# Two-layer convolutional attention on one Trainium2 core: layer 1's last product from seven block products, and its scores in five PSUM banks a unit

## The chip, the cores and the metric

The kernel runs on one core of one Trainium2 chip, in one launch. The metric is the device time of the launch in microseconds (us). Three runs of the kernel before took 3203.37, 3204.1 and 3202.24 us; the median is 3203.37. The five engines that the profile names are PE (TensorE, matmuls), DVE (VectorE), ACT (ScalarE), POOL (GpSimd) and SP (SyncE, which here only issues DMAs). Matmul results land in PSUM, whose banks hold 512 float32 numbers in each of 128 partitions.

## The reference

The input x has 8 images of 512 channels and 32 × 32 = 1024 positions, all float32. Two layers run one after the other; image by image they are:

```
# layer 0
h = group_norm(x)                                # 32 groups
q, k, v = split(w_qkv h + b_qkv)                 # 8 heads of 64 channels
a = softmax((q k) / sqrt(64)) v                  # 1024 x 1024 in each head
x = x + group_norm(w_proj a + b_proj)
# layer 1, weights normalized row by row
qkv = w_qkv x
q, k, v = split(qkv / (sqrt(mean(qkv^2 over channels)) + 1e-4))
attn = softmax(q k / sqrt(512))                  # one head, 1024 x 1024
x = (x + w_out (attn v)) / sqrt(2)
```

The change is all in layer 1's two large products: the scores q·k, and the last product, attn times (w_out v).

## The kernel before

**Stages.** The images go one after the other through the same stages, and one image's last stage is drawn into the next one's first. Layer 0 of an image is 32 steps (`STEPS`, line 370), each a block of 128 rows in two heads. `Heads.step` (line 636) orders a step: two maxima on DVE and two exponentials on ACT (`softmax`), the values of an earlier step, the **fills** (PE work of something else, as functions in a list), the scores of the next step, the transposition of the last step's exponentials on DVE with its four DMAs on SP (`turn`), the **earlies**, the reciprocal and POOL's scaling (`scale`), the **laters**. Then come the output projection and its group norm (`finish_layer0`), and layer 1 (`Layer1`, line 921). The weights of q and k are folded into one matrix ("score"), those of w_out and v into another ("value"), once at the start.

**Layer 1.** `Layer1.project` makes, in this order: products with the Gram matrix for the norms; u = score matrix times x (two `score_unit`s); v = (value matrix times x) turned (four `value_unit`s); and the exponentials of the scores, e (four `weight_unit`s). All matmuls of these units are 512 (value: 256) columns wide and 128 rows deep. The tiles e[0] and e[1] hold the two halves of the 1024 query positions, with eight blocks of 128 key positions each. POOL adds the exponentials up in `esum`. After `project` come the column totals (`square_sums`, `total`: a transposition, a small matmul, a reciprocal, and a round trip through DRAM on SP) and the last product, which is scaled by the reciprocal totals and added to x (`keep`).

**Seven block products.** Every unit computes a 2 × 2 block product from seven products of block sums in place of eight (class `Seven`, line 759). The sums on the left are S1 to S4, on the right T1 to T4 (`RightSide`, line 722). Each product is two calls of PE.matmul that accumulate in one PSUM bank, four MATMUL instructions in the trace. Two products share one two-bank tile from the pool `ps_s` (three tiles, `wide`, line 111); when the second is done, both are drained, by copies on ACT or additions on DVE into the result. The other pool, `ps_m`, has two single banks (`bank`, line 114). A unit of scores has seven drains on DVE and one on ACT; then ACT takes the exponential in place.

**The last product** is a plain one: for each half `th` of the positions and each block `c` of 128 channels, eight PE.matmuls of 512 columns (`products`, line 1096). The half 0 and block 0 of half 1 run before the next image's first scores; blocks 1, 2 and 3 of half 1 are the fills of the next image's steps 0, 1 and 2, with their `keep`s as laters (lines 1447 and 1448). Blocks 2 and 3 are made in 64-row halves into two banks (`products_rows`, line 1105), since the scores of layer 0 around them are 64-row matmuls too; `keep` joins the halves with a copy on ACT and two operations on POOL.

**Order.** `InOrder` (line 26) pins every instruction to program order on its engine, so the engines run exactly what the program lists, in that order. That is why every instruction in the profile has line L34, and groups are told apart by tiles: `p_e_B` and `p_e_T` are the PSUM tiles of the weight units, `po<-e,v` is the last product, `s<-qk` layer 0's scores, `pq` the projections of q and k. Waits between engines are put in by the framework from the tiles that are read and written.

**Around the change.** `project_seven` (line 476) makes q and k of a head pair of layer 0 in pieces, as fills; its products use the small banks too. Its weights come by `fetch_qk` (line 257) into the tile `qk7`, issued on SP: j = 1 and 2 after the score units (lines 1058 to 1060), j = 3 and 4 at steps 8 and 16. `Sums` (line 434) builds the sums for it, on DVE, one a product of weight units 1 to 3 (lines 1073 to 1076). The input of the image after next is loaded (`load_x`) and its group norm is reckoned between the parts of the last product (lines 1410 to 1443).

Of the kernel before, what the change touches and what calls it, by code (L numbers as in the profile page):

```python
# [13 lines left out]
P = 128  # L14
# [38 lines left out]
def attention_blocks_kernel(  # L53
# [157 lines left out]
    def rsqrt(r, v, n, name):  # L211
# [6 lines left out]
        "qk": ("qk", [P, 2, CI, C]), "score": ("qk", [P, 7, 2, CH]), "qk7": ("qk", [P, 2, 14, P]),  # L218
# [27 lines left out]
    def place(name, b):  # L246
        tag, shape = places[name]
        near[name] = weights.tile(shape, F32, tag=f"w_{tag}", name=f"{name}_{b}")
        if name == "v":

            near["v7"] = near[name]
            flat = near[name].rearrange("p k h c -> p (k h c)")
            near["v#"], near["v_"] = flat[:, CI * C :], flat[:, : CI * C]
            near[name] = flat[:, : CI * C].rearrange("p (ci c) -> p ci c", ci=CI)
        return near[name]

    def fetch_qk(j, b):

        if j == 1:
            place("qk7", b)  # L260
# [215 lines left out]
    def project_seven(b, j, right):  # L476
# [3 lines left out]
        qk = pair.tile([P, 2, N], F32, tag="qk", name=f"qk_{b}_{j}")  # L480
        kp = qk[:, 1, :].rearrange("p (be m) -> p be m", be=4)
# [5 lines left out]
        q1, q2 = (qk[:, 0, th * HN : (th + 1) * HN] for th in range(2))  # L487
        k1, k2 = (kp[:, :, th * P : (th + 1) * P] for th in range(2))

        def add(to, a, b_):  # L490
            return lambda: PO.tensor_add(to, a, b_)

        adds = (
            ([], []),
            ([], []),
            ([add(q2, q2, q1), add(k2, k2, turned(q2))], [add(k1, k1, k2), add(k2, k2, turned(tmp[1]))]),
            ([add(q1, q1, tmp[0]), add(q2, q2, tmp[1])], [add(q2, q2, tmp[2])]),
        )

        def pieces():  # L500
# [3 lines left out]
            yield adds[0]  # L504
# [17 lines left out]
        return qk, pieces()  # L522
# [398 lines left out]
    class Layer1:  # L921
# [10 lines left out]
        def project(self, hn_next):  # L932
# [96 lines left out]
            def weight_unit(m):  # L1029
# [7 lines left out]

                c = {f"{th + 1}{i + 1}": e[th][:, m + 4 * i, :] for i in range(2) for th in range(2)}

                def last(which):  # L1040
                    th, t = int(which[0]) - 1, m + 4 * (int(which[1]) - 1)
                    et, esum = c[which], self.sums[:, halves_[th]]
                    AC.activation(et, et, AF.Exp, bias=shift, scale=rinv[:, t : t + 1])
# [6 lines left out]
                return Seven(f"e_{b}_{m}", HN, left, self.right(slice(m * P, (m + 1) * P)), c, last, swap=True)  # L1050

            done = ([], [])
            for m in range(2):
                for k, _ in enumerate(score_unit(m).steps()):
                    if (m, k) == (0, 3):
                        roots()
                        broadcast()
            if b + 1 < B:
                for j in (1, 2):
                    fetch_qk(j, b + 1)  # L1060
# [6 lines left out]
            more = iter(())  # L1067
            if b + 1 < B:
                place("v", b + 1)
                self.next = Sums(b + 1, hn_next)  # L1070
                more = self.next.steps()
                next(more)
            for m in range(4):
                for _ in weight_unit(m).steps():
                    if m:
                        next(more, None)
            Seven.drain()
            Seven.half = None
            slots.give(f"u_{b}")

# [7 lines left out]
        def total(self):  # L1088

            pe = ps_s.tile([P, SQ], F32, tag="sc", name=f"pe_{self.b}")  # L1090
# [5 lines left out]
        def products(self, th, c, between=None, po=None):  # L1096
            po = self.po[th, c] = bank(f"po1_{self.b}_{th}_{c}") if po is None else po
            e = self.e[th]

            terms = [(self.v[:, t, c * P : (c + 1) * P], e[:, t, :]) for t in (0, 4, 1, 5, 2, 6, 7, 3)]  # L1100
            for k, _ in enumerate(matmuls(po, terms)):
                if k == 1 and between:
                    between()

        def products_rows(self, c):


            pos = self.po[1, c] = [bank(f"po1_{self.b}_1_{c}_{r}") for r in range(2)]
            for t in range(NT):
                for r in range(2):  # L1110
                    rows = halves[r]
                    PE.matmul(
                        pos[r],
                        self.v[rows, t, c * P : (c + 1) * P],
                        self.e[1][rows, t, :],
                        start=(t == 0),
                        stop=(t == NT - 1),
                    )

        def keep(self, th, c):  # L1120

            hs = slice(th * HN, (th + 1) * HN)

            po, rest = self.po.pop((th, c)), None
            if isinstance(po, list):
                po, rest = po
            share = near["v#"][:, N : N + HN] if self.b + 1 < B else po
            VE.tensor_mul(share, po, self.sums[:, hs])
            VE.scalar_tensor_tensor(self.xt[:, c, hs], self.xt[:, c, hs], 2.0 ** -0.5, share, ALU.mult, ALU.add)
            if rest is not None:  # L1130
                part = near["v#"][:, :HN]
                AC.copy(part, rest)
                PO.tensor_mul(part, part, self.sums[:, hs])
                PO.tensor_add(self.xt[:, c, hs], self.xt[:, c, hs], part)
            if th == 1:
                SY.dma_start(out=ov[self.b, :, c, :], in_=self.xt[:, c, :])

        def last_piece(self, c, cols):

            hs, po = slice(HN + cols.start, HN + cols.stop), bank(f"po1_{self.b}_1_{c}_{cols.start}", HN // 2)  # L1140
            run(matmuls(po, [(self.v[:, t, c * P : (c + 1) * P], self.e[1][:, t, cols]) for t in range(NT)]))
            VE.tensor_mul(po, po, self.sums[:, hs])
            VE.scalar_tensor_tensor(self.xt[:, c, hs], self.xt[:, c, hs], 2.0 ** -0.5, po, ALU.mult, ALU.add)
            SY.dma_start(out=ov[self.b, :, c, hs], in_=self.xt[:, c, hs])
# [134 lines left out]
    laters = [[] for _ in range(CI)]  # L1279
    heads.scores(0)  # L1280
    for b in range(B):
        hn, more = heads.hn, b + 1 < B
        todo, due, rest = iter(()), [], []
        for i in range(STEPS):
# [12 lines left out]
            if i < CI:  # L1297
                fill, later = fills[i] + fill, laters[i]
# [3 lines left out]
            if r == 0:  # L1302
                if j + 1 < CI:
                    heads.qk[j + 1], todo = project_seven(b, j + 1, one.next.right) if b else project_rows(
                        b, j + 1, hn, near["v#"]
                    )
# [30 lines left out]

            if b and i == NB:
# [78 lines left out]
        one.square_sums()  # L1417

        for c in range(CI):
            if c % 2 == 0:  # L1420
                po = wide(f"po1_{b}_0_{c}")
            one.products(0, c, norm_step if c == CI - 1 else None, po[:, c % 2])
            if c == 0:
                one.total()
                if b + 2 < B:
                    for ci in range(2, CI):
                        load_x(b + 2, hn_next, ci)
            if c and b + 2 < B:

                for ci in range(CI)[2 * c - 2 : 2 * c]:  # L1430
                    for k in range(2):
                        norm1.stats(ci, k)
                if c == 2:
                    norm1.aggregate()
            if c == CI - 1:
                norm_step()
            if c % 2:
                one.keep(0, c - 1)
                one.keep(0, c)
        slots.give(f"e_{b}_0")  # L1440
        if more:
            one.products(1, 0, norm_step)
            run(steps)
            one.keep(1, 0)
# [50 lines left out]
```

## Time and profile before

| what | value |
|---|---|
| median of three runs | 3203.37 us (3202.24 to 3204.1) |
| span of the profiled execution | 3197.2 us |
| instructions in it | 36929 |
| one weight stage (four units), image 0 | 404 to 452 us |
| its last product before the next scores | 452 to 487 us |
| the next image's steps 0 to 3 | from 487 us |

The times of steps come from one profiled execution, whose span is a little shorter than the time of a run. A line of a timeline has the start in us, the length in us, the engine, the line, the operation, the tile that it writes and (after the arrow) the tiles that it reads, its shape, and how many instructions are drawn together; in brackets stands how long the engine had been idle before it, and which engine ended that. A line of the costliest groups has the sum of the busy time, the mean of one in ns, and the idle time just before them with what ended most of it. A row of the windows has the stretch, its length, the busy time of PE, weight load, DVE, ACT and POOL (instructions in brackets), the granted PE clock (1.00 is full), the share of the DMA engines, and GB/s. On one engine, the time from one start to the next is the price of an instruction in a row; its length in the trace includes a tail that overlaps with the next.

### The profile page before, as it was taken

How to read it: one execution, taken by the hardware profiler on the slowest of the kernel's cores; microseconds unless marked ns; L12 is line 12 of the kernel's file. 1: busy time of each engine (PE TensorE's matmuls, PEld its weight loads, DVE VectorE, ACT ScalarE, POOL GpSimd, SP SyncE). 2: the span in 40 equal slices, each digit the busy share in tenths (PEclk: the TensorE clock that was granted, in tenths of full speed). 3: DMA queues.
4: the chain of work that ended last, by engine and by line, in shares of the span. 5: the costliest groups of instructions: out<-in, count | busy, mean ns of one | idle time of the engine just before them, and what ended most of it. 6: DMA issues, size and time to landing. Idle time of an engine off the chain costs nothing.

```text
span 3197.2 us, 36929 instructions
## 1 busy us (share of the span) xinstructions
PE 3172.7 (99%) x13374; PEld 1639.4 (51%) x13374; DVE 2286.3 (72%) x3175; ACT 1044.1 (33%) x1810; POOL 1269.7 (40%) x1033
## 2 busy tenths in 40 slices
PE   9999999999999999999999999999999999999899
PEld 5455644556444554445544555445554456444454
DVE  5697767866678766886658866687666877578753
ACT  2453124521145211551215512254023531245310
POOL 1554225732267212761226603366224642246121
PEclk9999999999999999999999999999999999999999
DMA  6777225862268511884128832388224872158600
GB/s 204 209 204 221 76 56 156 220 199 60 56 179 234 178 40 60 210 229 146 48 82 220 225 116 46 112 217 230 93 56 118 218 225 76 30 152 215 191 7 33
DMA packets 225853, 451.59 MB, mean 141 GB/s; under 512 B 21604, under 2 KB 62344, under 8 KB 219912
## 3 DMA queue, kind: packets, MB, share of 16 engines
q1 hardware_dynamic: 225552, 449.20, 50.1%
q8 instruction: 107, 1.75, 0.2%
q14 instruction: 74, 0.61, 0.1%
q10 hardware_dynamic: 120, 0.02, 0.0%
HBM read 137.26 MB, written 29.56 MB: 52 GB/s over the span
## 4 chain that ended last, share of the span: by engine, by line
PE 95%; DMA 2%; DVE 1%; SPq 1%; POOL 1%; issue 0%; ACT 0%; DVEq 0%; POOLq 0%
PE po L34 27%; PE s L34 14%; PE pq L34 7%; PE p_e_T L34 7%; PE p_v_T L34 6%; PE p_e_B L34 5%; PE p_v_B L34 5%; PE pqk L34 5%; PE py L34 4%; PE p_u_T L34 3%; PE p_o_T L34 3%; PE p_u_B L34 3%; PE p_o_B L34 2%; DMA pT<-pb 1%; PE pv L34 1%; PE pG L34 1%
## 5 line engine op out<-in xcount | busy, mean ns | idle before, releaser
L34 POOL TENSOR_SCALAR p<-p,tt 128x1024 f32<-128x1024 f32 x512 | 567.6, 1122 | 728.1 <-DVE tt L34 718.5
L34 ACT ACTIVATE p<-s,nm 128x1024 f32<-128x1024 f32 x512 | 566.2, 1111 | 821.8 <-DVE nm L34 498.4
L34 DVE TENSOR_REDUCE nm<-s 128x1 f32<-128x1024 f32 x512 | 602.5, 1218 | 147.3 <-PE s L34 146.5
L34 DVE STREAM_TRANSPOSE pb<-p 128x2048 f32<-128x2048 f32 x256 | 589.9, 2304 | 39.5 <-DMA pT<-pb 21.6
L34 PE MATMUL s<-qk 64*128 64x512 f32 x2048 | 501.9, 603 | 0.2
L34 PE MATMUL po<-pT,v 128*64 128x256 f32 x4096 | 473.4, 382 | 2.7 <-DMA pT<-pb 2.6
L34 PE MATMUL po<-e,v 128*128 128x512 f32 (+2 forms) x1264 | 449.5, 588 | 0.0
L34 PEld LDWEIGHTS po<-pT,v 128*64 128x64 f32 x4096 | 283.7, 137 | 228.4 <-issue 27.3
L34 PEld LDWEIGHTS po<-e,v 128*128 128x128 f32 (+1 forms) x1264 | 196.3, 189 | 233.9 <-issue 233.1
L34 PEld LDWEIGHTS s<-qk 64*128 64x128 f32 x2048 | 191.6, 186 | 235.5 <-issue 216.7
L34 PE MATMUL pq<-hn,qk 64*128 64x512 f32 (+1 forms) x420 | 191.8, 593 | 0.0
L34 POOL TENSOR_TENSOR esum<-esum,e 128x512 f32<-128x512 f32 x96 | 130.5, 1361 | 154.3 <-ACT e L34 151.8
L34 POOL TENSOR_TENSOR x<-x,o 128x1024 f32<-128x1024 f32 x21 | 52.2, 2514 | 348.9 <-ACT o L34 348.9
L34 POOL TENSOR_TENSOR u<-u,xy 128x512 f32<-128x512 f32 x64 | 79.2, 1270 | 278.6 <-DMA xy<-far_rinv 274.1
L34 ACT ACTIVATE e<-e,shift,rinv 128x512 f32<-128x512 f32 x128 | 101.1, 814 | 256.5 <-DVE e L34 256.5
L34 DVE TENSOR_TENSOR e<-e,p_e_T 128x512 f32<-128x512 f32 x160 | 107.0, 685 | 86.4 <-PE p_e_T L34 84.2
L34 DVE TENSOR_TENSOR v<-v,p_v_T 128x256 f32<-128x256 f32 x300 | 114.4, 419 | 68.9 <-PE p_v_T L34 49.9
L34 PE MATMUL pqk<-hn,qk 64*128 64x512 f32 (+1 forms) x672 | 158.2, 590 | 0.0
L34 PE MATMUL pq<-v,qk 64*128 64x512 f32 x336 | 150.9, 589 | 0.0
L34 PE MATMUL pq<-t,qk 64*128 64x512 f32 x336 | 150.9, 589 | 0.0
L34 PE MATMUL p_e_T<-s,t 128*128 128x512 f32 x320 | 147.8, 592 | 0.0
L34 PE MATMUL py<-x,gram 128*128 128x512 f32 x320 | 141.6, 602 | 4.4 <-DVE x L34 4.4
(224 smaller groups left out, 4116.5 us busy)
## 6 DMA issues: line engine op xcount, KB each, us to landing
pT<-pb SPq DMA_DIRECT2D x1024, 256.0 KB, 4.5
qk<-far_qk SPq DMA_DIRECT2D x21, 896.0 KB
hn<-in_x_dram SPq DMA_DIRECT2D x32, 512.0 KB, 4.5
x<-in_x_dram SPq DMA_DIRECT2D x32, 512.0 KB, 3.7
out_dram<-x SPq DMA_DIRECT2D x31, 512.0 KB, 3.1
score<-far_score SPq DMA_DIRECT2D x8, 1792.0 KB
value<-far_value SPq DMA_DIRECT2D x8, 1792.0 KB
proj<-far_proj SPq DMA_DIRECT2D x7, 1792.0 KB
```

The costliest lines, as they stand in the source:

```text
L34: return lambda *args, **kw: self._pin(call(*args, **kw))
```

## The change

**The weight units** no longer use `Seven`. A unit has tiles x and y of two banks each and z, of which it uses one bank: five banks. Its seven products, in PE's order, and what reads them:

1. A11·B11 into x0; 2. S1·T1 into x1; then ACT copies x0 to c12.
3. S2·T2 into y0; 4. S3·T3 into y1; then DVE adds c12 += y0, c21 = c12 + y1, c22 = c21 + x1, and ACT takes the exponential of c22.
5. A12·B21, accumulated on x0, which the copy has read.
6. A22·T4 into z0; ACT takes the exponential of x0 straight into c11.
7. S4·B22, accumulated on x1, which the third addition has read; DVE adds c21 += z0 and c12 += x1, each followed by its exponential.

**The last product** is made from seven block products too, for each of two column blocks m and with four calls each: A11·B11, A12·B21 (accumulated on the first), S2·T2 and S3·T3 before the next image's scores (`first_products`), S1·T1, A22·T4 and S4·B22 as fills of steps 0, 1 and 2 (`last_products`). All are 128 rows deep. The block sums of e and v for it are made in place or in borrowed tiles: on DVE in the weight units (`right_sums`, two 512-column sums a unit, and two of v in unit 0), and on POOL and DVE between the products. Partial results lie in the unused half of `qk7`. The additions of the partial products are laters of steps 0, 1 and 2, POOL scales them by the reciprocal totals, and the results are added to x in the earlies of steps 1, 2 and 3.

**What moves with it.** `qk7` is filled for j = 2 at step 4, in place of right after j = 1. The q/k tile of `project_seven` is taken with its second piece, handed over by the callback `made`. The loads of x for the image after next are issued before `total`. The last image runs `finish`, whose last product is cut into 512 and twice 256 columns.

In the built program PE has 6556 matmul calls in place of 6736, DVE 3259 instructions in place of 3183, POOL 1094 in place of 1044, ACT 1305 in place of 1303 and SP 1322 in place of 1321. Of the 180 calls that go, 64 are whole ones of 512 columns and 128 rows; 112 go since blocks are no longer cut into 64-row halves, and 4 since less is cut in the last image.

The core of the diff (the class `Layer1` and what calls it):

```diff
@@ Layer1.project, weight_unit @@
-                return Seven(f"e_{b}_{m}", HN, left, self.right(slice(m * P, (m + 1) * P)), c, last, swap=True)
+                x_, y_ = wide(f"pe_{b}_{m}_x"), None
+                product(x_[:, 0], A11, "B11")
+                yield
+                product(x_[:, 1], S1, "T1")
+                AC.copy(c["12"], x_[:, 0])
+                yield
+                y_ = wide(f"pe_{b}_{m}_y")
+                product(y_[:, 0], S2, "T2")
+                yield
+                product(y_[:, 1], S3, "T3")
+                add(c["12"], c["12"], y_[:, 0])
+                add(c["21"], c["12"], y_[:, 1])
+                add(c["22"], c["21"], x_[:, 1])
+                last("22")
+                yield
+                product(x_[:, 0], A12, "B21", first=False)
+                yield
+                z_ = wide(f"pe_{b}_{m}_z")
+                product(z_[:, 0], A22, "T4")
+                last("11", x_[:, 0])
+                yield
+                product(x_[:, 1], S4, "B22", first=False)
+                add(c["21"], c["21"], z_[:, 0])
+                last("21")
+                add(c["12"], c["12"], x_[:, 1])
+                last("12")
+                yield
...
-                for _ in weight_unit(m).steps():
+                for k, _ in enumerate(weight_unit(m)):
                     if m:
                         next(more, None)
+                        if k == 3:
+                            self.right_sums(m - 1)
+                    elif k == 2:
+                        VE.tensor_sub(self.vs3, v[:, :4, :CH], v[:, :4, CH:])
+                    elif k == 5:
+                        VE.tensor_add(v[:, :4, CH:], v[:, :4, CH:], v[:, 4:, CH:])
...
+        def right_sums(self, m):
+            e0, e1 = self.e
+            VE.tensor_sub(self.et3[:, m], e1[:, m + 4], e1[:, m])
+            VE.tensor_sub(e1[:, m], e1[:, m], e0[:, m])
...
+        def product(self, pm, a, b_, m, first=True, cols=slice(0, HN), between=None):
+            (l, l0, lc), (r, r0) = self.operand(a, m), self.operand(b_, m)
+            for h in range(4):
+                PE.matmul(pm, l[:, l0 + h, lc], r[:, r0 + h, cols], start=first and h == 0, stop=h == 3, skip_group_check=True)
...
+        def first_products(self, after):
+            (e0, e1), v, parts, b = self.e, self.v, self.parts, self.b
+            pa = [bank(f"pa_{b}_{m}") for m in range(2)]
+            self.right_sums(3)
+            for m in range(2):
+                self.product(pa[m], "A11", "B11", m)
+                AC.copy(parts[:, m, 0], pa[m])
+                PO.tensor_sub(
+                    v[:, :4, m * P : (m + 1) * P], v[:, :4, CH + m * P : CH + (m + 1) * P], v[:, :4, m * P : (m + 1) * P]
+                )
+            self.square_sums()
+            after(0)
+            for m in range(2):
+                self.product(pa[m], "A12", "B21", m, first=False)
+                if m == 0:
+                    VE.tensor_sub(e0[:, :4], e1[:, 4:], e1[:, :4])
+                    self.total()
+            PO.tensor_sub(v[:, 4:, :CH], v[:, 4:, :CH], v[:, :4, :CH])
+            after(1)
+            p2 = wide(f"p2_{b}")
+            for m in range(2):
+                self.product(p2[:, m], "S2", "T2", m)
+            for m in range(2):
+                VE.tensor_add(parts[:, m, 0], parts[:, m, 0], p2[:, m])
+            p3 = wide(f"p3_{b}")
+            self.product(p3[:, 0], "S3", "T3", 0, between=lambda: after(2))
+            for m in range(2):
+                self.keep(0, m, pa[m])
+            self.product(p3[:, 1], "S3", "T3", 1, between=lambda: after(2))
+            for m in range(2):
+                VE.tensor_add(parts[:, m, 1], parts[:, m, 0], p3[:, m])
+            PO.tensor_sub(self.et3, e0[:, 4:], e0[:, :4])
+            after(3)
...
@@ the main loop @@
-            fills = [[lambda c=c: (one.products_rows(c) if c > 1 else one.products(1, c))] for c in range(1, CI)] + [[]]
-            laters = [[lambda c=c: one.keep(1, c)] for c in range(1, CI)] + [[]]
+            products, adds, keeps = one.last_products()
+            fills = products + [[]]
+            laters = [[f] for f in adds] + [[]]
+            earlies = [[]] + [[f] for f in keeps]
...
+            if b and i == CI:
+                fetch_qk(2, b)
```

In `last_products`, one product makes a pair of banks, and its additions read them twice or once; in `finish`, the last piece of S4·B22 takes the bank of the first:

```diff
+            def add_5():
+                for m in range(2):
+                    VE.tensor_add(spare[m], parts[:, m, 1], pm[5, m])
+                    self.scaled(1, spare[m])
+                    VE.tensor_add(parts[:, m, 0], parts[:, m, 0], pm[5, m])
...
+            for m, n in ((0, HN), (1, HN // 2)):
+                for c0 in range(0, HN, n):
+                    po, hs = bank(f"po_{b}_6_{m}_{c0}", n), slice(HN + c0, HN + c0 + n)
+                    self.product(po, "S4", "B22", m, cols=slice(c0, c0 + n))
+                    VE.tensor_mul(po, po, sums[:, hs])
+                    VE.tensor_add(xt[:, m, hs], xt[:, m, hs], po)
+                    SY.dma_start(out=ov[b, :, m, hs], in_=xt[:, m, hs])
```

## The prediction

> **What bounds the kernel now.** I read the page's head and busy shares, then the chain that ended last, then the costliest groups and PE's waits, and last the timeline of one unit of layer 1's scores and of the first softmax step of an image.
>
> ```profile
> span 3197.2 us, 36929 instructions
> PE 3172.7 (99%) x13374; PEld 1639.4 (51%) x13374; DVE 2286.3 (72%) x3175; ACT 1044.1 (33%) x1810; POOL 1269.7 (40%) x1033
> ...
> PE 95%; DMA 2%; DVE 1%; SPq 1%; POOL 1%; issue 0%; ACT 0%; DVEq 0%; POOLq 0%
> ...
> L34 POOL TENSOR_TENSOR esum<-esum,e 128x512 f32<-128x512 f32 x96 | 130.5, 1361 | 154.3 <-ACT e L34 151.8
> ...
> L34 DVE TENSOR_TENSOR e<-e,p_e_T 128x512 f32<-128x512 f32 x160 | 107.0, 685 | 86.4 <-PE p_e_T L34 84.2
> ```
>
> PE is busy 3172.7 of 3197.2 us: it stands still for 24.5 us in all, and 95% of the last chain is its own. So PE's program order is the time. A matmul that goes is worth its full length, and a wait put in front of a matmul costs its full length, whatever the other engines have to spare. The profiled execution's span is 3197.2 us; the median of the three runs, 3203.4, is 6.2 us above it. I add the change to both alike.
>
> One unit of layer 1's scores before (start, us, engine):
>
> ```profile
> 403.90 1.88 PE L34 MATMUL p_e_B<-u,x 128*128 128x512 f32 x4
> ...
> 405.62 1.88 PE L34 MATMUL p_e_B<-s,t 128*128 128x512 f32 x4
> 407.33 1.88 PE L34 MATMUL p_e_T<-s,t 128*128 128x512 f32 x4
> 407.59 0.59 ACT L34 COPY e<-p_e_B 128x512 f32<-128x512 f32 x1 [1.17 <-PE p_e_B L34]
> ...
> 409.05 1.88 PE L34 MATMUL p_e_T<-u,t 128*128 128x512 f32 x4
> 410.77 1.88 PE L34 MATMUL p_e_T<-s,t 128*128 128x512 f32 x4
> 410.97 1.41 DVE L34 TENSOR_TENSOR e<-e,p_e_T 128x512 f32<-128x512 f32 x2 [2.07 <-PE p_e_T L34]
> ```
>
> Here the reader sees three prices. A block product (two PE.matmul calls, four MATMUL instructions) starts every 1.717 us (405.62 − 403.90, and so on), so one call of 512 columns is 0.858 us. DVE's first add starts 0.20 us after the point where PE could start its next product (410.97 − 410.77). And waits go by the whole two-bank tile: the first bank of p_e_B is complete at 405.78, ACT is idle for 1.17 us, yet its copy out of that bank starts at 407.59, just behind the product into the second bank (405.62 + 1.88 = 407.50).
>
> **What goes.** The last product takes 7 × 2 × 4 = 56 calls an image in place of 64: 8 × 8 images × 0.858 = **−54.9 us**. Halving a call into two 64-row parts, as before for two of the four c, cost nothing by the trace, so undoing it gains nothing. The score units keep 14 calls. DVE loses two adds a unit; PE doesn't wait for them now, so that is worth 0.
>
> **What comes: the fifth product.** In PE's new order A12·B21, which accumulates on x0, stands straight behind S3·T3. The order of the changed program gives its first matmul two waits: ACT's copy of x0, long done, and the *third* of the chained adds (c12 += y0, c21 = c12 + y1, c22 = c21 + x1), since that add reads bank x1 of the same tile. All 32 units have this. The first add can't start before S3·T3 ends, as that is the last write to tile y. Behind the waiting matmul PE has A22·T4 and S4·B22, which could run earlier but stand in line. The stall is: 0.20 to the first add; two chained adds at 0.72 each (pair above: 2 × 0.69 in 1.41, 0.72 from start to start); the third add 0.69; then back to PE. For the way back:
>
> ```profile
> 3007.27 0.47 ACT L34 ACTIVATE a<-po,cols 128x256 f32<-128x256 f32 x1 [7.68 <-PE po L34]
> ...
> 3007.79 1.12 PE L34 MATMUL pp<-a,proj 128*128 128x512 f32 x2 [0.56 <-ACT a L34]
> ```
>
> PE starts 0.05 us after the releaser's end, and the first matmul after a stop takes some 0.10 us longer than one in a row (0.53 against 0.429 from start to start). Sum 0.20 + 1.44 + 0.69 + 0.05 + 0.10 = 2.48 us, × 32 = **+79.5 us**. Bounds: 2.2 us (adds back to back at 0.69 with no restart cost; 70 in all) and 3.0 us (96) where adds lag. I take 2.48, the rows themselves. The other waits of a unit are covered: S4·B22 waits for the exp of c11, about 1.0 us behind its product, under the 1.72 of A22·T4; the next unit's third product waits for the z add, which has 1.5 us to spare.
>
> **New work on VectorE in units 1 to 3**: per unit two 128x512 sums (right_sums), among the sums of the next image that stand there already. They come behind the three adds and have the 6.9 us of four products. They are late only if Pool slows them:
>
> ```profile
> 426.62 3.25 DVE L34 TENSOR_TENSOR hn<-hn 64x512 f32<-64x512 f32 x2
> ```
>
> ```profile
> 426.38 2.95 POOL L34 TENSOR_TENSOR esum<-esum,e 128x512 f32<-128x512 f32 x2 [5.54 <-ACT e L34]
> ```
>
> These two DVE sums take 1.6 us each beside Pool's, against 0.68 alone. The units have room for one such pair; I take 2 us in all, bounds 0 and 1.5 us in 21 units = 31.
>
> **Step 0 of the next image.** Before:
>
> ```profile
> 487.06 1.99 PE L34 MATMUL s<-qk 64*128 64x512 f32 x8
> ...
> 488.98 7.13 PE L34 MATMUL po<-e,v 128*128 128x512 f32 x16
> ...
> 489.08 2.36 DVE L34 TENSOR_REDUCE nm<-s 128x1 f32<-128x1024 f32 x2 [0.49 <-PE s L34]
> ```
>
> Now two S1·T1 products (8 calls, 6.87 us) fill both small banks, and the query product behind them waits until DVE has read the first twice. DVE does the two part adds of S3·T3 first (1.4 us) and a dozen small normalization instructions at 0.2 us, so its first maximum starts 4.0 us after the scores begin; its reciprocal comes 3.64 later (492.72 − 489.08), and the two adds end at 9.2 us. PE is there at 1.92 + 6.87 = 8.79. With the restart 0.5 us, in the 6 images that still normalize a later one: **+3.0** (bounds 0 and 9).
>
> **Steps 1 and 2**: the fills are now 128-row matmuls between 64-row scores; a switch costs 0.10 us (486.54 to 487.06 is 0.52 against 0.429). Two a fill, two fills, 7 images: **+2.8**.
>
> **The end.** In the last image S4·B22's third piece waits for the bank of the first: DVE first finishes the A22·T4 parts (behind Pool's scaling, 1.36 us each) and four adds for S4's first half: some 5.9 us behind A22·T4, then 1.4 for its own two, against PE at 3.43 + 1.72 = 5.15. **+2.2**.
>
> **Nothing** for the rest: the copies of the A11·B11 parts (0.59) lie under 3.43 us of products; the 2048-element sum on e0 and Pool's sums on v end before their readers' turn; the reciprocal sums (esum) arrive some 4 us before need. On SP, the loads of x are issued a little earlier and the second qk load goes to step 4, behind four transposes' DMAs, one step ahead of its use; it costs up to 0.3 us an image if late. The pair buffer that et3 holds delays only the next query tile, which is now taken at step 3.
>
> Sum: −54.9 + 79.5 + 2 + 3.0 + 2.8 + 2.2 = **+34.6 us**. Span 3197.2 → 3231.8; run time 3203.4 → **3238**.
>
> [...] The wait on the x tile is the program's; the chip might not need it. [...] The row at 407.59 decides: the program waits by tile.
> [...]
>
> **Rivals.**
> 1. *The fifth product isn't held by the adds* (faster). If waits went by bank, only the copy would stand before it, and the sum would be −54.9 + 10.0 = −44.9: 3158. It decides at a stall of 44.9/32 = 1.40 us a unit: held by one add only (0.20 + 0.69 + 0.15 = 1.04) gives 3192, by two (1.76) 3215. For it: two banks are separate memory. Against: the program's wait and the copy at 407.59. Chance 0.09 (0.05 none, 0.02 one, 0.02 two).
> 2. *PE's clock falls in the stalls.* In the windows (PEclk before the last two columns):
>
> ```profile
> 2478.00:2480.00 2.00, 0.99 (x8) 0.57 (x8) 1.30 (x2) 1.93 (x5) 0.47 (x1) 1.00 0.86 253
> 3012.00:3015.00 3.00, 0.00 (x0) 0.00 (x0) 2.86 (x7) 0.00 (x0) 0.00 (x0) 0.79 1.02 435
> ...
> 3024.00:3027.00 3.00, 3.00 (x5) 1.16 (x4) 2.96 (x6) 1.74 (x3) 0.00 (x0) 0.50 0.00 0
> ```
>
> A 1.29-us gap (2478) leaves 1.00; a 3.83-us gap from 3011.5 ends at 0.50, and it stays there for 5.6 us of work. 2.5 lies between. If each stall did this, 2.8 us more × 32 = +90: 3328. Chance 0.05.
> 3. *VectorE becomes the bound in the score units*: the adds start 1 to 1.5 us late in 21 units: +21 to +31, 3259 to 3269. For it: DVE is 72% busy on average and 1.6-us sums stand in those units. Against: 6.9 us of room. Chance 0.08.
>
> **Numbers.** Forecast 0.78, with its own range 3219 (stall 2.2 and none of the smaller items: 3203.4 − 54.9 + 70.4) to 3259. The range takes in rival 3: 3219 to 3269; 0.05 lies above it, 0.09 below, the rest for errors of size. About 0.2%, 6.4 us, is what a measurement of this kernel can tell from no change: faster 0.07 (rival 1 with none or one add), same 0.03, slower 0.90.
>
> **What will show it.** PE's idle time up from 24.5 to about 110 us, with a wait of PE on DVE for the p(e) x tile in 32 places of 2.3 to 2.5 us; 13014 MATMUL instructions; granted clock still 1.00 in the score stage. Wrong if that stage is no longer than before (48.0 us, 404 to 452, for the first image), if its waits name ACT, or if its clock is under 1.

## The result, and the profile after

The changed kernel took 3326.95 us (median of four runs, 3321.53 to 3333.47) against 3202.8 before (four runs): 1.039 times as long, 95% interval 1.0373 to 1.0409. The forecast was 3238, with a range to 3269. The side was right; the loss is 124 us and not 35.

The page of the changed kernel, the lines that answer to those of before:

```profile
span 3330.4 us, 36481 instructions
...
PE 3186.3 (96%) x13014; PEld 1624.1 (49%) x13014; DVE 2393.8 (72%) x3251; ACT 1047.2 (31%) x1812; POOL 1377.9 (41%) x1083
...
PE 85%; DVE 7%; DMA 3%; SPq 2%; ACT 1%; issue 1%; POOL 1%; DVEq 0%; POOLq 0%; ACTq 0%
```

PE is idle for 144.1 us (3330.4 − 3186.3) in place of 24.5, so 119.6 of the span's 133.2 us more are waits. But PE is also *busy* 13.6 us longer, although calls worth 54.9 us are gone: the work that is left takes 68.5 us more. The two have to be looked for in different views. PE's waits (what waited, for what; us in all, times, longest):

```profile
PE pe_x L34 <- DVE e L34: 76.3, 32, 2.4
PE pq L34 <- DVE qk L34: 16.5, 6, 2.8
PE po L34 <- DMA pT<-pb: 13.9, 9, 2.8
PE s L34 <- POOL qk L34: 13.4, 7, 2.2
...
PE po L34 <- DVE x L34: 2.1, 1, 2.1
```

The first line is the fifth product, once in each of the 32 units. The second is the query product of step 0, the third and fourth stand in steps 5 to 8 of each image, the fifth is the end. Against before (2.6 us in the third line, none in the others) they make the 119.6 us. One unit in the timeline:

```profile
409.94 1.41 DVE L34 TENSOR_TENSOR e<-e,pe_y 128x512 f32<-128x512 f32 x2 [3.37 <-PE pe_y L34]
411.39 0.69 DVE L34 TENSOR_TENSOR e<-e,pe_x 128x512 f32<-128x512 f32 x1
...
412.22 1.96 PE L34 MATMUL pe_x<-u,x 128*128 128x512 f32 x4 [2.39 <-DVE e L34]
```

Three additions in a row, and PE's next product 0.14 us behind the third: 2.39 us idle.

The busy time is explained by the clock. The windows below are cut at multiples of 3.413 us, where the trace's clock records have their edges (columns: stretch, length, busy time of PE, weight load, DVE, ACT, POOL, then the granted clock, DMA share, GB/s):

```profile
424.93:428.34 3.41, 1.48 (x4) 0.80 (x5) 3.24 (x6) 0.81 (x1) 0.64 (x1) 1.00 0.00 0
428.34:431.75 3.41, 3.41 (x10) 1.50 (x9) 3.41 (x3) 0.78 (x1) 2.24 (x2) 1.00 0.74 154
438.58:441.99 3.41, 1.02 (x3) 0.30 (x2) 2.70 (x5) 0.60 (x1) 0.00 (x0) 1.00 0.00 0
441.99:445.40 3.41, 3.41 (x5) 1.35 (x4) 2.73 (x3) 0.80 (x2) 1.33 (x1) 0.50 0.00 0
445.40:448.81 3.41, 3.41 (x9) 1.52 (x8) 0.81 (x2) 1.00 (x2) 1.49 (x2) 1.00 0.76 159
```

The stall of the second unit is cut by a window's edge, so that 1.93 us of it fall in one window: the next window has the full clock and 10 matmuls. The third unit's 2.39 us fall in one window whole: the next has half the clock and 5 matmuls in the same busy time. Half-clock time sums to 122.2 us in the records of this run, 14.8 before; half of the difference, 54 us, is lost. That leaves some 15 us for restarts behind about 60 stops (0.1 us each, as in the row of before at 3007.79), tile-shape switches (0.10 us each, by the rows of before at 486.54 and 487.06), and what I can't place. These sums are of the profiled execution, whose span is 133.2 us longer; the medians differ by 124.

### The profile page after: what moved, and what is told of

Same layout as the page of the kernel before. It is cut to its first block, busy times and chain, and to the rows that moved or that the text cites. A ratio compares the mean times of both kernels' runs of the same rounds, so it can differ in the third digit from the quotient of the medians.

```text
span 3330.4 us, 36481 instructions
## 1 busy us (share of the span) xinstructions
PE 3186.3 (96%) x13014; PEld 1624.1 (49%) x13014; DVE 2393.8 (72%) x3251; ACT 1047.2 (31%) x1812; POOL 1377.9 (41%) x1083
## 4 chain that ended last, share of the span: by engine, by line
PE 85%; DVE 7%; DMA 3%; SPq 2%; ACT 1%; issue 1%; POOL 1%; DVEq 0%; POOLq 0%; ACTq 0%
PE po L34 15%; PE s L34 12%; PE pe_x L34 7%; PE p_v_T L34 6%; PE pq L34 5%; PE p_v_B L34 5%; PE py L34 4%; PE pqk L34 4%; PE p L34 3%; PE pa L34 3%; PE p_u_T L34 3%; PE pe_y L34 3%; PE p_o_T L34 3%; DMA pT<-pb 3%; PE p_u_B L34 2%; PE p_o_B L34 2%
## 5 line engine op out<-in xcount | busy, mean ns | idle before, releaser
L34 PE MATMUL s<-qk 64*128 64x512 f32 x2048 | 513.3, 615 | 13.6 <-POOL qk L34 13.4
L34 POOL TENSOR_TENSOR esum<-esum,e 128x512 f32<-128x512 f32 x96 | 133.2, 1390 | 245.1 <-ACT e L34 245.1
L34 PE MATMUL pe_x<-u,x 128*128 128x512 f32 x256 | 144.8, 695 | 76.3 <-DVE e L34 76.3
L34 PE MATMUL pq<-hn,qk 64*128 64x512 f32 (+1 forms) x420 | 195.8, 603 | 16.5 <-DVE qk L34 16.5
L34 ACT ACTIVATE e<-e,shift,rinv 128x512 f32<-128x512 f32 x96 | 77.6, 813 | 263.0 <-DVE e L34 263.0
L34 POOL TENSOR_TENSOR esum<-e 128x512 f32<-128x512 f32 x16 | 23.7, 1482 | 297.5 <-ACT e L34 297.5
L34 POOL TENSOR_TENSOR qk<-qk,v 128x512 f32<-128x512 f32 x96 | 127.0, 1332 | 3.2 <-ACT v L34 1.6
L34 DVE TENSOR_TENSOR e<-e,pe_y 128x512 f32<-128x512 f32 x64 | 44.0, 687 | 110.1 <-PE pe_y L34 109.0
```

The costliest lines, as they stand in the source:

```text
L34: return lambda *args, **kw: self._pin(call(*args, **kw))
```

## The experiments

Theory A: a window of 3.41 us in which PE is idle for 2 us or more is followed by one at half clock, and the stalls of the units are long enough for that. Theory B: the stalls cost their own length, and the clock has other causes. Besides, each further wait has its own theory, below. All times are medians; "stage" is the time from an image's first score product to the next image's first scores, by the trace (83.2 us before, 91.8 in the changed kernel, in most images).

| run | what | us | against before (interval) | stage |
|---|---|---|---|---|
| e1 | fifth product held by two additions | 3272.5 | 1.0222 (1.0207 to 1.0238) | 83.9 |
| e12 | held by four (one run) | 3369.1 | | |
| e2 | x0, x1 in single banks | 3234.0 | 1.0107 (1.0090 to 1.0124) | 79.9 |
| e7 | e2, DVE's sums in another order | 3209.4 | 1.0026 (1.0017 to 1.0036) | 76.3 |
| e3 | new last product alone | 3235.8 | 1.0108 (1.0090 to 1.0127) | 80.4 |
| e4 | new units alone | 3316.0 | 1.0358 (1.0342 to 1.0373) | 97.0 |
| e5 | group-norm instructions later | 3297.5 | 1.0298 (1.0281 to 1.0315) | |
| e10 | Pool's subtraction in four (one run) | 3317.1 | | |
| e6 | second load at step 6 | 3304.6 | 1.0319 (1.0303 to 1.0336) | |
| e8 | e7, e5 and e6 together | 3170.5 | 0.9902 (0.9887 to 0.9917) | 76.3 |
| e9 | e8, load in four parts, other end | 3172.1 | 0.9904 (0.9887 to 0.9920) | 76.3 |
| e11 | e8, six sevenths of the load out | 3165.8 | 0.9888 (0.9871 to 0.9904) | |
| e13 | e8, stores out | 3162.0 | 0.9882 (0.9867 to 0.9896) | |
| e14 | e8, both out | 3152.7 | 0.9855 (0.9840 to 0.9869) | 76.3 |
| e15 | e8, stores one a step, other end | 3191.0 | 0.9967 (0.9955 to 0.9978) | |
| e16 | e15, load between the stores | 3195.9 | 0.9987 (0.9978 to 0.9997) | |
| e17 | e8, load at step 5, other end | 3181.3 | 0.9936 (0.9923 to 0.9950) | 76.3 |

**The stall and the clock: e1 and e12.** The edit of e1, with which the second addition reads x1:

```diff
                 add(c["12"], c["12"], y_[:, 0])
+                add(c["22"], c["12"], x_[:, 1])
                 add(c["21"], c["12"], y_[:, 1])
-                add(c["22"], c["21"], x_[:, 1])
+                add(c["22"], c["22"], y_[:, 1])
```

> The changed kernel, but DVE reads bank x1 in the second of its additions (c22 = c12 + x1, then c21 = c12 + y1, then c22 += y1), so the fifth product waits for two additions and not three. Theory A: a 3.41-us window of TensorE's clock in which PE is idle for 2 us or more is followed by one at half clock; a stall of 2.4 us can do that, one of 1.67 us can't. Then 32 x 0.72 = 23 us of waits go, and with them the 22 or so half-clock windows that follow the units' stalls, 1.7 us each = 38 us: 3327 - 61 = 3266, and the clock in the units stays at 1.00. Theory B: the clock has other causes than these stalls; then only the 23 us go: 3304.

3272.5, 54 us less, for 22.7 us of waits less. The wait of a unit is 1.66 us (2.02 in one), and no half-clock window follows any of the 32. The line of the waits, and then a stretch of 3.41 us around one of the stalls (PE is busy 1.75 us of it, so idle for 1.66):

```profile
PE pe_x L34 <- DVE e L34: 53.6, 32, 2.0
```

```profile
424.00:427.41 3.41, 1.75 (x5) 0.57 (x4) 2.36 (x4) 0.00 (x0) 0.00 (x0) 1.00 0.00 0
```

A is right, B (3304) is not. e12 goes the other way, with an addition more in front (`add(c["22"], c["21"], y_[:, 1])`):

> The changed kernel with one more addition in front of the one on x1 (its result is overwritten), so that the fifth product waits 3.1 us and not 2.39. Theory (a half-clock window of 3.41 us follows each window in which PE is idle for 2 us or more): waits 76 + 23 = 99 us; more of the 32 stalls leave 2 us in one window, 24 to 32 in place of 22, so 3327 + 23 + 3 to 17 = 3353 to 3367. Rival (the clock falls for as long as PE was idle): 3327 + 23 + 16 or more, with half-clock stretches of other lengths than 3.41 us.

3369.1 in one run, with 99.7 us of waits; 34 separate half-clock windows have exactly 3.41 us, two 6.83. About 29 of the 32 stalls are followed by one, in the changed kernel 22. That is A's side, a little above its numbers.

I summed PE's idle time, from the trace's matmul records, in each 3.413-us window with the full clock, in the changed kernel and the 17 others. In 230 windows the next one is at half clock: PE was idle in them for 1.96 us or more (once 1.88). Where the next one has the full clock, no window has over 2.01, from the first clock record on (12 us into the span of the changed kernel). So the edge is at about 2.0 of 3.41 us, and whether a stall of 2.4 us costs 2.4 or 4.1 us depends on where the grid, the edges of these windows, cuts it. Of the same 32 stalls of 2.38 us, 22 are followed by a half-clock window in the profiled execution of the changed kernel and in e10's, 16 in those of e4, e5 and e6. The four executions of the changed kernel fit this, with a mean clock of 0.982 in the two of 3332 and 3333 us, and of 0.986 and 0.985 in the two of 3322.

**What holds the fifth product: e2 and e7.**

```diff
-                x_, y_ = wide(f"pe_{b}_{m}_x"), None
+                x_, y_ = [bank(f"pe_{b}_{m}_x{k}") for k in range(2)], None
...
```

> The changed kernel, but x0 and x1 are two single banks of the small pool in place of one two-bank tile. Theory A (the third addition holds the fifth product only because x0 and x1 share a tile, and the stall drops the clock): 76 us of waits, some 3 us of restarts and 38 us of half clock go: 3327 - 117 = 3210. Theory B (waits, but not the clock): 3327 - 79 = 3248. If something else than the shared tile holds the fifth product, it stays near 3327.

3234.0. The 2.39-us stalls and their half clock are gone, so it was the shared tile that held the fifth product. In the first unit it now starts before the additions:

```profile
409.79 1.88 PE L34 MATMUL pe_x<-u,x 128*128 128x512 f32 x4
...
410.06 1.41 DVE L34 TENSOR_TENSOR e<-e,pe_y 128x512 f32<-128x512 f32 x2 [3.36 <-PE pe_y L34]
...
411.50 0.69 DVE L34 TENSOR_TENSOR e<-e,pe_x 128x512 f32<-128x512 f32 x1
411.50 1.88 PE L34 MATMUL pe_z<-u,t 128*128 128x512 f32 x4
...
413.00 0.76 ACT L34 ACTIVATE e<-pe_x,shift,rinv 128x512 f32<-128x512 f32 x1
413.22 1.88 PE L34 MATMUL pe_x<-s,x 128*128 128x512 f32 x4
```

By these rows TensorE accumulates on x0 while DVE reads the banks of y, writes z0 while DVE reads x1, and accumulates on x1 while ACT reads x0, and its products still start 1.71 to 1.72 us apart; the hold was the program's. But a new wait has come, 20.6 us in 14 units (here the second unit's; PE's next product into x1 waits for DVE's last addition on the x1 before):

```profile
427.00 2.36 DVE L34 TENSOR_TENSOR hn<-hn 64x512 f32<-64x512 f32 x2
429.29 0.67 DVE L34 TENSOR_TENSOR e<-e,pe_z 128x512 f32<-128x512 f32 x1
429.88 0.67 DVE L34 TENSOR_TENSOR e<-e,pe_x 128x512 f32<-128x512 f32 x1
...
430.61 1.99 PE L34 MATMUL pe_x<-s,t 128*128 128x512 f32 x4 [1.77 <-DVE e L34]
```

DVE works off sums for the next image in front of the additions. e7 puts them, and `right_sums`, behind a unit's last addition (one sum a unit still stands right behind the three chained ones):

```diff
-                    if m:
-                        next(more, None)
-                        if k == 3:
-                            self.right_sums(m - 1)
+                    if k == 6 and m in (1, 2):
+                        self.right_sums(m - 1)
+                    if (m, k) == (3, 0):
+                        self.right_sums(2)
+                    if m and k not in (4, 5) or (m, k) == (0, 6):
+                        next(more, None)
+                    if (m, k) == (0, 6):
+                        next(more, None)
```

> The single-bank version (3234), with DVE's other sums moved: the block sums of e and the next image's sums stand behind a unit's last addition, where DVE has 6 us, and not between its additions. Theory: the 20.6 us that PE still waits in 14 units (first product into x1, for the last addition on x1) are DVE working off those sums at 1.6 us each beside Pool; they go: 3234 - 20 = 3214. Rival: DVE has too little room in any order: the waits come back in front of the third addition or in front of the last product, 3234.

3209.4, and PE has no wait left in the units. The stage takes 76.3 us, 6.9 less than before: 8 calls × 0.858 us, to the tenth.

**One part alone: e3 and e4.** e3 has the old units (`Seven`) with the new last product, e4 the reverse.

> The new last product alone, with the weight units of before (eight-bank seven-product units with seven additions). Theory A: near e2, 3210, that is 7 us slower than before in spite of 55 us less of matmuls: 16.5 (query product of step 0) + 11 (DMA of step 5) + 13 (scores behind Pool) + 2 (end) of new waits, some 15 us of half clock behind them, and a dozen of restarts and tile-shape switches give it back. Theory B: the last product gains what its calls save less the waits, 3203 - 55 + 43 + 5 = 3196.

> The new weight units alone, with the last product of before. Theory A: 3203 + 76 + 3 + 38 = 3320, nearly all that the whole change costs. Theory B: 3203 + 79 = 3282.

e4 confirms A (3316.0). e3 missed both of its numbers (3210 and 3196): at 3235.8 it is as slow as e2, for another reason. Besides the waits of steps 0 to 8 it has 15.2 us, in front of the last product's first matmul (2.2 us an image), for ACT's last exponential of the old unit, which takes A12·B21 last. So neither part gains by itself as written; the calls saved are real, and the last product's own waits eat them.

**Step 0: e5 and e10.** Here is the query product's wait in the changed kernel:

```profile
493.09 1.29 DVE L34 TENSOR_TENSOR qk<-qk,p 128x512 f32<-128x512 f32 x2 [1.46 <-PE p L34]
493.14 4.51 POOL L34 TENSOR_TENSOR et<-e 128x2048 f32<-128x2048 f32 x1 [11.77 <-PE p L34]
494.30 3.38 DVE L34 SCALAR_TENSOR_TENSOR rs<-a 128x4 f32<-128x4 f32 x1
494.90 7.13 PE L34 MATMUL po<-e,v 128*128 128x512 f32 x16
497.71 0.16 DVE L34 TENSOR_TENSOR rs<-rs,ve 128x4 f32<-128x4 f32 x1
...
499.75 2.35 DVE L34 TENSOR_REDUCE nm<-s 128x1 f32<-128x1024 f32 x2
```

A DVE instruction on four columns takes 3.38 us and ends at 497.68, when Pool's ends at 497.65; its like take 0.16. It is so in all six images that have it. DVE's maximum comes 4.85 us late, and the query product with it. e5 moves the instructions into step 0's laters (`laters[0].append(lambda steps=steps: run(steps))`); e10 leaves them and cuts Pool's subtraction in four.

> The changed kernel, with the eleven small group-norm instructions on DVE (128 x 4) moved from ahead of step 0's first maximum to step 0's laters, behind the additions of S1*T1. Theory: in step 0 the query product waits 2.75 us since one of these instructions took 3.38 us, until Pool's 2048-element subtraction beside it ended, and the rest 2.2 us; so DVE's first maximum starts 4.85 us after PE has begun the S1*T1 products. Moved, it starts right behind the scores, the 16.5 us of waits go, and four half-clock windows with them: 3327 - 16.5 - 7 = 3303. Rival: the query product waits for the additions behind the reciprocal as such; then the wait falls to a third, 3316. Rival 2: the small instructions meet Pool's scaling in their new place and step 1's maximum comes late: no gain, 3327.

> The changed kernel, with Pool's 2048-element subtraction at the end of the first products cut into four of 512. Theory: a small DVE instruction beside it is held until Pool's instruction ends (3.38 us in place of 0.16, ending at the same time as Pool's 4.51 us). Cut, it is held for at most one part, some 1.1 us, and further small instructions are held at the next parts; the chain of eleven ends no later, and the query product's wait of 2.75 us shrinks by up to 2 us in 6 images: 3327 - 12 or less. Rival: the slow one is slow whatever Pool does: it still takes 3.4 us, 3327.

e5: 3297.5, and the wait of 16.5 us is gone whole; neither rival holds. The gain is 29.5 us, more than the theory's 24; that six fewer of the units' stalls are followed by half clock in its trace, by the luck of the grid, would make up for the difference. e10: 3317.1 in one run, with the wait down to 4.3 us. Its trace:

```profile
490.92 5.47 POOL L34 TENSOR_TENSOR et<-e 128x512 f32<-128x512 f32 x4 [8.96 <-PE p L34]
...
494.88 0.31 DVE L34 SCALAR_TENSOR_TENSOR rs<-a 128x4 f32<-128x4 f32 x1
495.22 1.19 DVE L34 TENSOR_TENSOR rs<-rs,ve 128x4 f32<-128x4 f32 x1
```

No small instruction is held longer than 1.19 us now, about one part of Pool's (four in 5.47 us). In e5 the same instructions meet another Pool operation in their new place, and one of them takes 0.85 us and ends with it, six times of six. So in these runs they are held until Pool's instruction ends: for 3.38 us beside 4.51 (ends at 497.68 and 497.65), and in e10 for 1.19 beside the last of the four parts (496.41 and 496.39).

**Steps 5 to 8: e6, e8, e9, e11 and e13 to e17.** Of the changed kernel, SP's queue in steps 2 to 5 (the length is that of the whole group of issues), and what comes of it:

```profile
525.68 2.71 SPq L34 DMA_DIRECT2D out_dram<-x  x2
531.32 3.25 SPq L34 DMA_DIRECT2D pT<-pb  x4
534.67 2.02 SPq L34 DMA_DIRECT2D out_dram<-x  x2
536.78 1.36 SPq L34 DMA_DIRECT2D qk<-far_qk  x1
...
549.29 2.31 DVE L34 STREAM_TRANSPOSE pb<-p 128x2048 f32<-128x2048 f32 x1 [4.43 <-DMA pT<-pb]
549.41 3.67 PE L34 MATMUL po<-pT,v 128*64 128x256 f32 x32 [1.79 <-DMA pT<-pb]
...
555.26 1.99 PE L34 MATMUL s<-qk 64*128 64x512 f32 x8 [2.17 <-POOL qk L34]
```

In steps 2 to 4, 2 MB of stores and the 896 KB of weights stand beside 1 MB of exponentials a step. DVE's transposition of step 5 waits 4.43 us for its DMAs, PE's values 1.79; behind DVE, Pool's q/k sums are late, and the scores of step 8 wait 2.17 us. From 536.5 to 547 us the 16 DMA engines are 97% busy in the mean. e6 moves the load (`if b and i == CI + 2`).

> The changed kernel, with the second load of q/k weights (896 KB) issued at step 6 in place of step 4. Theory: in steps 3 and 4 this load and the stores of x (4 x 512 KB) share the queue and the DMA engines with the transposed exponentials, which land late; DVE's transposition and the values of step 5 wait for them, and Pool's sums for q/k come late behind that. Then 11.3 us of PE's waits on DMA, 13.4 us of its waits on Pool, and five half-clock windows go: 3327 - 25 - 8 = 3294. Rival: the stores alone do it, or the q/k tile that is taken later: no change, 3327.

3304.6, a gain of 22 us and not 33: 20 of the 27 us of such waits stay, 8.5 of them now of the query product for the load itself. In the profiled executions most of the gain is clock: 19 falls to half clock in place of 33, and six of the 14 that are gone stood behind the units' stalls, which this edit leaves as they are. e8 puts e7, e5 and e6 together:

> The three last together: x0 and x1 in single banks with the new order of DVE's sums, the group-norm instructions in step 0's laters, and the load at step 6. If the costs add up: 3214 - 24 - 33 = 3157, below before (3201) by what the 64 calls save (55) less the end (2), the switches (3) and a few restarts. If they take each other's place, 3190 to 3214.

3170.5: **1.0% faster than before**, the best of the runs that leave nothing out, though 13 us above the sum. Some of what e5 and e6 gained alone was half clock behind the units' stalls, which e7 takes out too, so the sum counts that part twice. PE still waits 22 us in these steps:

```profile
PE pq L34 <- DMA qk<-far_qk: 8.1, 6, 2.1
PE s L34 <- POOL qk L34: 7.9, 7, 1.9
PE po L34 <- DMA pT<-pb: 6.2, 7, 1.2
```

e9 cuts the load into four, and gives the last image's last pieces two-bank tiles (`wide(...)[:, 0, :n]`), which takes the end's 2.1 us away:

> e8 with the second load of q/k weights cut in four (256, 256, 192 and 192 KB), issued at steps 4 to 7, and with the last image's three S4*B22 pieces in two-bank tiles, so that the third needn't wait for the first's reader. End: 2.1 us of wait and a half-clock window of 1.7 go. Load: in e8 PE still waits 22 us behind DMAs in steps 5 to 8. If one burst of 896 KB in the queue is what makes the transposed exponentials late, the small parts hide and some 18 us go: 3170 - 4 - 18 = 3148. If the DMA engines have no room at all in these steps (1 MB in each, 5.2 us long), the same bytes make the same delay wherever they stand: 3166.

3172.1, no gain: Pool's line grows to 12.3 us, and the steps of the eight images together are no shorter (1615 us from the first scores to the output projection, 1613 in e8). e11, e13 and e14 leave traffic out:

> e8 with six sevenths of the second load of q/k weights left out (128 KB of 896 KB, at step 4; the head pair that would use them gets other numbers). Theory: it is this load, in steps that already move 1 MB each in 5.2 us, that costs PE's 22 us of waits behind DMAs and Pool in steps 5 to 8, wherever it stands; without it they fall to the 2.6 us of before, and 3170 becomes 3150. Rival: the stores of x (2 MB in steps 2 and 3, where before spread them over steps 0 to 2) make the exponentials late; then it stays above 3163.

> e8 with the 2 MB of stores of each finished image but the last left out (steps 2 and 3). Theory S: the four stores, two at a time in steps of 9 and 5 us that also move 1 MB of exponentials each, make the transpositions late (DVE waits 29.5 us for these DMAs in e8, 21.6 before), and Pool's q/k sums behind them; without them PE's 22 us of waits in steps 5 to 8 fall to some 10, what the load alone costs: 3158. Theory P: these waits are Pool's own lateness in steps 0 to 3 (its scaling of the products) and don't depend on the DMAs: 3170.

> e8 without those stores and without six sevenths of the load. If DMA traffic is the whole cause of the waits in steps 5 to 8, stores and load together, they go: 3170 - 20 = 3150. If Pool or DVE is late by itself, it stays where e11 is, 3166.

Without six sevenths of the load 3165.8, without the stores of all images but the last 3162.0, without both 3152.7, and then these three lines are gone but for 0.3 us. So the waits are DMA traffic, all of it: without the stores the time falls by 8.5 us, without the load by 5, without both by 18. My theory of e11, that it is the load, was wrong; Pool and DVE are not late by themselves. The last three try other places for the same bytes. In e15 and e16 the stores of blocks 2 and 3 of the last image are not made, and the buffer of x comes free later, with the last store.

> e8 with the stores of a finished image issued one a step (steps 2, 3, 4, 5), the load after them at step 6, and the last image's S4*B22 pieces in two-bank tiles. Theory S: 4 us at the end and about half of the 22 us go: 3156. Theory P: only the 4 us: 3166.

> As e15, but two stores at steps 2 and 3, the load at step 4, and the other two stores at steps 6 and 7. If only the amount in any one step matters, as e15, 3156; if the load must not stand close behind the first scores of the next head pair (step 8), better than e15 by the 8 us that the query product waits for it in e8: 3150.

> e8 with the second load at step 5 in place of 6, and the last image's S4*B22 pieces in two-bank tiles. End: 2.1 us of wait and its half-clock window go. Load one step earlier: the 8 us that the query product waits for it in step 8 go, the waits on the exponentials' DMAs and on Pool (14 us in e8) grow by up to as much. 3170 - 4 - 0 to 8 = 3158 to 3166.

All three missed. In e15 the load comes after all the stores and lands late: the query product waits 31.3 us for it. In e16 DVE waits 65.8 us for exponentials (29.5 in e8), PE 18.3 behind them and 14.6 behind Pool. In e17 the listed waits are fewer than in e8, yet the time is 11 us longer, in the steps (205.7 us an image from the first scores to the output projection, by the mean of the second to the seventh, 204.4 in e8, 200.8 before). It can be seen as busy time, in score groups such as this one, which takes 3.12 us in place of 1.99:

```profile
541.29 3.12 PE L34 MATMUL s<-qk 64*128 64x512 f32 x8
...
542.43 0.30 PEld L34 LDWEIGHTS s<-qk 64*128 64x128 f32 x4 [0.85 <-ACT p L34]
```

Its second half stands behind a late exponential of ACT while the first half still runs, and the list of PE's waits doesn't show such a wait. From each start to the next, layer 0's scores take 492.1 us in e17 and 480.8 in e8, of which 8.1 are the query product's wait: 19 us more, against 9 us of listed waits less. Why ACT is late there stays open. Before had this load between layer 1's units (338 to 404 in the first image), where the DMA engines were 21% busy; none of the places in the steps that were tried is free.

## Why the prediction was wrong

- **The calls that go, −54.9.** Right: the stage of e7 and e8 is shorter by 6.9 us, eight calls an image.
- **The fifth product, +79.5.** Right: 76.3 of idle time and the restarts, by the three chained additions, in all 32 units. That the program waits by tile was right, and e2 shows that only the program's tile made the wait.
- **The clock: the step that failed.** Rival 2 said that "A 1.29-us gap (2478) leaves 1.00; a 3.83-us gap from 3011.5 ends at 0.50" and that "2.5 lies between", and got a chance of 0.05. Two points with 2.5 us between them bound nothing. The row of 3012 to 3015 even said more: a mean of 0.79 over 3 us is 1.26 us at half clock, so the clock fell at about 3013.7, when PE had been idle for some 2.2 us, less than the 2.48 of a stall. By that row the rival should have been near an even chance at least. What happened is that rival, in part: 22 of the 32 stalls, and some ten of the other waits, are followed by a half-clock window. Its price was off too, 2.8 us a stall against 1.7 (half of 3.41); the 5.6 us of half clock that I read came behind a longer stop. In all about 54 us that the sum did not have. That the rival's 3328 is what was measured is luck: 90 us of clock too many by 36, against 38 us of waits in the steps that it left out. The prediction's own sign of being wrong, a clock under 1 in the score stage, came (0.50 in 441.99 to 445.40). That a stall of 2.48 us leaves the clock alone, so that the sum has no term for it, was an estimate that no run shows: about 2.0 us of idle time in one window of 3.413 us were enough in every run here.
- **Step 0, +3.0.** Mis-sized: 16.5 of waits, and half clock behind most of them. The reason was in the right place, DVE's first maximum, but of the "dozen small normalization instructions at 0.2 us" one took 3.38 beside Pool, and only the others 0.16. I priced the added Pool subtraction only by when it ends, not by whom it holds.
- **"It costs up to 0.3 us an image if late": the second step that failed.** Stores and load cost 24.7 us of waits, 3.5 an image; that both are the cause is shown on e8 (by e14), not on the changed kernel itself. I looked at the order on SP's queue and not at the bytes: 1 MB a step at 5.2 us a step is some 200 GB/s without them. Whether the engines' rate or the one queue's order sets the delay, no run separates.
- **VectorE late, +2; the end, +2.2.** In the changed kernel the stall itself gives DVE its time, so nothing shows; in e2, without the stall, it was 20.6. The end was 2.1.
- **Steps 1 and 2, +2.8.** No run has it alone; it lies in what I can't place.

The sum: 34.6 − 2 (VectorE, which didn't come) + 54 (clock) + 13.5 (step 0) + 24.7 (DMA) is 125. These terms are read from the profiled execution, which is 133 us longer than the one before, so some 8 us aren't placed; that the medians differ by 124 is no better a fit.

## What to carry to other kernels

A stall of PE had two prices here, its own length and, if it left about 2 us idle in one 3.41-us window, 1.7 us of half clock; so a wait cut from 2.4 to 1.7 us can give back more than twice what it is shorter (54 us for 22.7 in e1). If a matmul is to write on while another engine reads beside it, give the banks tiles of their own: in this program dependencies go by tile. A load moved from a quiet stage (DMA engines 21% busy) into one that streams (97%) was paid for in every place tried here, and a smaller matmul count is worth nothing until the waits around it are found one by one.

## What the runs showed of the hardware

- In these traces the granted clock fell for whole windows of 3.41 us, with edges at multiples of 3.413 us from one another. A window with PE idle for about 2.0 us or more was followed by one at half clock (230 windows of 18 kernels, the least idle 1.96 us but for one of 1.88), one with less was not (up to 2.01 us idle); a window at half clock in which PE was idle for less than 0.6 us was followed by a full one (in the changed kernel 33, with at most 0.31 us idle).
- A DVE instruction of 128 x 4 elements (`rs<-a`, 0.16 us otherwise) was held for 3.38 us beside a Pool subtraction, until that ended, six times of six (in e10, with Pool's work in four, for at most 1.19); two DVE additions `qk<-qk,p` that started within 0.05 us of the same subtraction were not (1.29 us for both; 1.41 for the pair at 409.94).
- TensorE accumulated in one bank while DVE or ACT read another, with no loss in the rows (e2: products 1.71 to 1.72 us apart, from 409.79).
